# Strip runs of the value product that go on from one key group to the next

## The chip, the cores and the metric

The kernel runs on one core of a Trainium2 chip. The metric is the time of one execution in microseconds (us), measured on the device; of several runs the median is given. A profiled execution of the same program gives the trace: start and duration of every instruction on TensorE (PE, with its weight loads as PEld), VectorE (DVE), ScalarE (ACT), GpSimd (POOL) and the queues of the DMA issuers (SP above all).

## The reference, cut to what matters

Two sequences of 1024 positions with 1024 features pass a feed-forward layer with eight low-rank experts, a causal attention layer, and the same feed-forward layer again, each behind a layer norm and added to its input:

```python
x = x + 0.5 * ffn(layernorm(x))
x = x + attn(layernorm(x))
x = x + 0.5 * ffn(layernorm(x))

# attn: 32 query heads of 32 features, 8 key/value groups, 4 query heads to a group
att    = einsum('bhgqd,bhkd->bhgqk', q, k) / sqrt(32)     # rotary positions on q and k
att    = where(causal, att, -inf)
probs  = softmax(att)
ctx    = einsum('bhgqk,bhkd->bhgqd', probs, v)
out    = ctx @ Wo
```

The change lies in `ctx`, the product of the probabilities with the values, and in the row sums of the softmax.

## The kernel before

Positions are cut into 16 tiles of 128, numbered t = 0 to 15, eight to a sequence. A query tile t meets L = t % 8 + 1 key tiles of its own sequence. The 8 key/value groups are handled in four pairs, an even group and the odd one after it. Tile 8 (LATE, with L = 1) is worked on last.

For a query tile and a group, `unit_s1` (L650, with a mask in L655 for small L) computes scores with queries on the partitions, and DVE takes row maxima (L667). For a pair of groups the maxima are folded into the query operand: for L above 3 by writing them to columns of `qst` (L687, L688) and transposing on the DMA queue of SP (`qt_load`, L630); for L up to 3 by a small matmul (L697) and a DVE multiply (L699). `unit_s2` then computes the scores a second time with keys on the partitions, one matmul for a key tile and the four heads of the group (L809, result `s2`, 128x512). ACT takes the exponential into one of eight buffers `p32` (L815), and POOL clears the half above the diagonal for the last key tile (L817). These fp32 tiles feed the value product.

The value product (L745) uses strips of the PE array: for each head of the group a 128x32 weight (the values of the group, or a column block of ones) is loaded into its own 32 columns of the array, and the head's 128x128 block of `p32` streams against it. The four heads' matmuls work side by side in the four column strips. I call these four matmuls a step; the trace shows each step as eight records, since an fp32 matmul is recorded twice. There are two kinds of step: with the values (`va`), one for each key tile; and with `ones`, which gives the row sums. To save `ones` steps, DVE first adds two `p32` tiles of the same group into a `pair` tile (L723), so that there is one `ones` step for two key tiles, and one for a key tile left over.

Steps are grouped in batches. `av_add` (L772) appends every exponential tile to the newest batch in `pend`; a batch is closed when it has four tiles (BATCH) or when the group changes. A batch is issued by `av_batch` (L726) once at least two tiles (SKEW) came after it: all its `va` steps first, from the newest tile to the oldest, then its `ones` steps. All its matmuls but the first are chained with `issue_after` and a high priority, which keeps most of a batch together on PE. The sums of a pair of groups lie in one PSUM tile `av` with a single buffer; after the pair's last batch `normalize` (L753) copies it out on ACT (L757) and DVE (L758 to L765) and writes the context rows, `tt`, with ACT (L767) and POOL (L768).

The dense layers (L409 to L411: three fp16 matmuls for the high and low halves, 128x512; L592 to L594 and L616 to L618 in the first tiles; L492 to L494 for the experts) are written as generators that the loops around `unit_s2` advance a piece at a time, so that dense work lies between the attention work. Their weights stream from DRAM into three `ws` buffers (L421), and their inputs come by DMA transposes (`tt<-hl`, L338). The final order on each engine is set by the framework's own planner, which starts from the order of the program, priorities and `issue_after`. PE, DVE, ACT, POOL and SP each then run their list in order.

With four tiles to a batch, closed at the end of each group, a query tile has 8 batches for L up to 4 and 16 for L from 5 to 8: 192 in all.

Of the kernel before, what the change touches and what calls it, by code (L numbers as in the profile page):

```python
# [9 lines left out]
FP = mybir.dt.float32  # L10
# [3 lines left out]
ALU = mybir.AluOpType  # L14
# [3 lines left out]
NH, NKV, DH, GRP = 32, 8, 32, 4  # L18
E, R = 8, 16
P = 128  # L20
KB = D // P
NT = B * T // P
TPB = T // P
# [7 lines left out]
BATCH = 4  # L31
# [13 lines left out]
def kernel(  # L45
# [16 lines left out]
    nc = tc.nc  # L62
# [42 lines left out]
    ones = const.tile([P, DH], FP)  # L105
# [432 lines left out]
    KT, VA, QS, CTX, CT = {}, {}, {}, {}, {}  # L538
# [166 lines left out]
    pend = deque()  # L705
    ready = {}
    avt = [None]

    pairs = {}

    def add_pairs(batch):

        t, g, L, us = batch
        key = (t, g, us[0][0])
        if key in pairs:
            return
        pairs[key] = []
        for i in range(0, len(us), 2):
            if i + 1 == len(us):
                pairs[key].append(us[i][1])  # L720
                continue
            sums = pp.tile([P, GRP, P], FP, name="pair", bufs=3)
            nc.vector.tensor_tensor(sums, us[i][1], us[i + 1][1], ALU.add)  # L723
            pairs[key].append(sums)

    def av_batch():  # L726

        add_pairs(pend[0])
        t, g, L, us = pend.popleft()
        odd = g % 2  # L730
        if us[0][0] == 0 and not odd:
            avt[0] = p_av.tile([P, 2, 2, P], FP, name="av")
        av = avt[0][:, odd]
        last = us[-1][0] == L - 1
        runs = [(0, VA[t - t % TPB + j][:, g, :], p32) for j, p32 in reversed(us)]
        runs += [(1, ones, sums) for sums in reversed(pairs.pop((t, g, us[0][0])))]
        prev = None
        for n, (i, w, p32) in enumerate(runs):
            for h in range(GRP):
                rows = slice(h * DH, (h + 1) * DH)  # L740
                with ExitStack() as st:
                    if prev is not None:
                        st.enter_context(tc.high_priority())
                        st.enter_context(tc.issue_after(prev.ins))
                    prev = nc.tensor.matmul(  # L745
                        av[rows, i, :], lhsT=w, rhs=p32[:, h, :],
                        start=(us[0][0] == 0 and n == 0), stop=(last and n == len(runs) - 1),
                        skip_group_check=True, tile_position=(0, h * DH),
                    )
        if last and odd:  # L750
            normalize(t, g - 1, avt[0])

    def normalize(t, g, av):  # L753

        w = pp.tile([P, GRP, P], FP, name="pair", bufs=3)
        o, rc = w[:, 0:2, :], w[:, 2:4, :]
        nc.scalar.copy(o, av[:, :, 0, :])  # L757
        nc.vector.transpose(rc, av[:, :, 1, :])  # L758
        r = small.tile([P, 2 * P // DH], FP, name="rcol")
        nc.vector.reciprocal(r, rc.rearrange("p a (b q) -> p (a b) q", q=DH)[:, :, 0])  # L760
        nc.vector.transpose(rc, r.unsqueeze(2).to_broadcast([P, 2 * P // DH, DH]))
        if t not in CTX:
            CTX[t] = Halves()
        c = CTX[t]
        nc.vector.tensor_tensor(o, o, rc, ALU.mult)  # L765
        hi, lo = c.tt[:, g : g + 2, :], c.tt[:, KB + g : KB + g + 2, :]
        nc.scalar.copy(hi, o)  # L767
        nc.gpsimd.tensor_tensor(lo, o, hi, ALU.subtract)  # L768
        if g == NKV - 2:
            CT[t] = CTX.pop(t)  # L770

    def av_add(t, g, j, L, p32):  # L772

        if not pend or len(pend[-1][3]) == BATCH or pend[-1][0:2] != (t, g):
            pend.append((t, g, L, []))
        pend[-1][3].append((j, p32))
        after = 0
        while len(pend) > 1:
            after = sum(len(b[3]) for b in list(pend)[1:])
            add_pairs(pend[0])  # L780
            if after < SKEW:
                break
            av_batch()
# [15 lines left out]
    def unit_s2(t, g):  # L799
        b0 = t - t % TPB  # L800
        L = t - b0 + 1
        odd = g % 2
        while ("q2", t, g - odd) not in Ts:
            turn_maxima()
        q = (Ts.pop if odd else Ts.get)(("q2", t, g - odd))[:, odd * GRP : (odd + 1) * GRP, :]
        cs = S["cs", g // 4]
        for j in range(L):
            ps = p_s2.tile([P, GRP, P], FP, name="s2")
            ins = nc.tensor.matmul(  # L809
                ps.rearrange("p h k -> p (h k)"), lhsT=KT[b0 + j][:, g, :],  # L810
                rhs=q.rearrange("p h k -> p (h k)"), start=True, stop=True,
            )
            s2_ins.append(ins.ins)
            p32 = pp.tile([P, GRP, P], FP, name="p32", bufs=8)
            nc.scalar.activation(p32, ps, AF.Exp, scale=cs)  # L815
            if j == L - 1:
                nc.gpsimd.affine_select(  # L817
                    out=p32, in_=p32, compare_op=ALU.is_ge, fill=0.0, base=0,
                    pattern=[[0, GRP], [1, P]], channel_multiplier=-1,
                )  # L820
            av_add(t, g, j, L, p32)
            yield

    def stage_c1(t):
        while t not in CT:
            av_batch()
        tt = CT.pop(t)
        xt = xts[t]
        for n in range(2):
            ps = p_dense.tile([P, 512], FP, name="pd")  # L830
            yield from dense_streamed(ps, tt, 3 + n)
            c = bass.ts(n, 512)
            nc.vector.scalar_tensor_tensor(xt[:, c], ps, S["uo", n], xt[:, c], ALU.mult, ALU.add)
            if n == 0:
                yield True
        Ts["x3", t] = layernorm(xt, turn=t in TURN3)
        yield True
# [103 lines left out]
    def flush(_):  # L941
        while pend:
            av_batch()
        yield True
# [144 lines left out]
    pp = ctx.enter_context(tc.tile_pool(name="pp", bufs=2, reuse_waits="tile"))  # L1089
# [69 lines left out]
```

## Time and profile before

| | |
|---|---|
| median of 3 runs | 1469.46 us (1466.78 to 1469.99) |
| profiled execution | 1466.47 us |
| its span in the trace | 1464.6 us |
| mean granted TensorE clock | 0.989 |
| PE / DVE / ACT / POOL busy | 95% / 74% / 49% / 25% of the span |
| strip matmuls (L745), records | 4608 with `va`, 2048 with `ones` on a `pair`, 512 with `ones` on a single tile |
| the same in steps of eight records | 576, 256 and 64 |
| DVE pair sums (L723) | 256, mean 708 ns |
| exponentials (L815) | 576, mean 687 ns |

A PE matmul's record is longer than the time to the next one, since matmuls are pipelined; what a matmul costs is the distance from its start to the start of the next. In a list of groups a row has the line, engine, operation, output and inputs, shapes, count, busy time, mean duration, and the idle time before it with what ended it. In a timeline a row has the start, the time covered, and how many records in a row were merged.

### The profile page before, as it was taken

How to read it: one execution, taken by the hardware profiler on the slowest of the kernel's cores; microseconds unless marked ns; L12 is line 12 of the kernel's file. 1: busy time of each engine (PE TensorE's matmuls, PEld its weight loads, DVE VectorE, ACT ScalarE, POOL GpSimd, SP SyncE). 2: the span in 40 equal slices, each digit the busy share in tenths (PEclk: the TensorE clock that was granted, in tenths of full speed). 3: DMA queues.
4: the chain of work that ended last, by engine and by line, in shares of the span. 5: the costliest groups of instructions: out<-in, count | busy, mean ns of one | idle time of the engine just before them, and what ended most of it. 6: DMA issues, size and time to landing. Idle time of an engine off the chain costs nothing.

```text
span 1464.6 us, 35179 instructions
## 1 busy us (share of the span) xinstructions
PE 1392.4 (95%) x14636; PEld 786.9 (54%) x14636; DVE 1084.9 (74%) x2416; ACT 720.2 (49%) x1233; POOL 369.3 (25%) x578
## 2 busy tenths in 40 slices
PE   5897999999999999999999899999999999999998
PEld 3443445555556555556554455555555555556544
DVE  6878768968678687787754686868778688789743
ACT  7574434535456455464541343545545455555521
POOL 3352223323222131221211232322222122221220
PEclk9998999999999999999999999999999999999999
DMA  8958397585875837935649759697794855933552
GB/s 303 278 178 197 105 258 200 118 275 147 235 205 102 277 92 180 256 75 166 199 122 290 187 151 262 158 258 185 177 270 66 258 132 106 276 75 88 131 160 85
DMA packets 254863, 266.75 MB, mean 182 GB/s; under 512 B 217072, under 2 KB 220144, under 8 KB 234992
## 3 DMA queue, kind: packets, MB, share of 16 engines
q1 hardware_dynamic: 248624, 237.25, 58.0%
q0 software_dynamic: 4640, 16.78, 6.5%
q10 hardware_dynamic: 1440, 10.49, 2.0%
q8 instruction: 114, 1.87, 0.5%
q14 instruction: 45, 0.37, 0.1%
HBM read 191.60 MB, written 20.45 MB: 145 GB/s over the span
## 4 chain that ended last, share of the span: by engine, by line
PE 76%; DVE 11%; DMA 7%; issue 1%; ACT 1%; POOL 0%; SPq 0%; DVEq 0%; ACTq 0%; POOLq 0%
PE pd L409 15%; PE pd L410 15%; PE pd L411 14%; PE av L745 12%; PE s L809 7%; PE s L650 7%; DVE mx L667 4%; DMA qt<-qst 3%; DMA ws<-wstr 2%; DMA tt<-hl 2%; DVE pair L723 2%; DVE bst L379 1%; DVE xt L496 1%; PE pd L492 1%; PE pd L592 1%
## 5 line engine op out<-in xcount | busy, mean ns | idle before, releaser
L815 ACT ACTIVATE p<-s,cs 128x512 f32<-128x512 f32 x576 | 381.3, 687 | 299.7 <-PE s L809 297.1
L667 DVE TENSOR_REDUCE mx<-s 128x4 f32<-128x512 f32 x480 | 316.0, 677 | 43.2 <-PE s L650 39.1
L723 DVE TENSOR_TENSOR pair<-p,p 128x512 f32<-128x512 f32 x256 | 180.5, 708 | 69.1 <-ACT p L815 36.0
L650 PE MATMUL s<-kts,qt 96*128 96x128 f16 x2304 | 217.2, 221 | 6.1 <-DVE mx L667 3.1
L809 PE MATMUL s<-qt,kts 128*128 128x512 f16 x576 | 211.3, 384 | 10.5 <-DMA qt<-qst 7.0
L650 PEld LDWEIGHTS <-qt 96*128 96x128 f16 x2304 | 164.7, 98 | 97.4 <-issue 28.2
L409 PE MATMUL pd<-ws,tt 128*128 128x512 f16 x544 | 207.1, 381 | 9.2 <-DMA ws<-wstr 7.0
L410 PE MATMUL pd<-ws,tt 128*128 128x512 f16 x544 | 206.7, 380 | 0.0
L411 PE MATMUL pd<-ws,tt 128*128 128x512 f16 x544 | 206.6, 380 | 0.0
L409 PE MATMUL pd<-wb,tt 128*128 128x512 f16 x512 | 196.0, 383 | 2.4 <-DVE xt L496 1.5
L409 PEld LDWEIGHTS <-tt 128*128 128x128 f16 x1312 | 129.1, 98 | 127.3 <-DMA tt<-hl 12.6
L410 PE MATMUL pd<-wb,tt 128*128 128x512 f16 x512 | 195.6, 382 | 1.1 <-DVE wb L217 1.1
L411 PE MATMUL pd<-wb,tt 128*128 128x512 f16 x512 | 195.7, 382 | 0.0
L411 PEld LDWEIGHTS <-tt 128*128 128x128 f16 x1312 | 129.0, 98 | 121.8 <-issue 5.5
L410 PEld LDWEIGHTS <-tt 128*128 128x128 f16 x1312 | 129.2, 98 | 120.7 <-issue 15.2
L817 POOL TENSOR_SCALAR_AFFINE_SELECT p<-p 128x512 f32<-128x512 f32 x128 | 91.5, 717 | 347.2 <-ACT p L815 347.1
L745 PE MATMUL av<-p,va 128*32 128x128 f32 x4608 | 166.6, 278 | 1.4 <-POOL p L817 1.4
L745 PEld LDWEIGHTS av<-p,va 128*32 128x32 f32 x4608 | 115.7, 110 | 59.5 <-issue 42.4
L662 POOL TENSOR_SCALAR_AFFINE_SELECT sm<-sm 128x512 f32<-128x512 f32 x96 | 67.4, 702 | 159.6 <-ACT sm L661 154.0
L745 PE MATMUL av<-pair,ones 128*32 128x128 f32 x2048 | 86.8, 276 | 1.3 <-DVE pair L723 1.2
L661 ACT COPY sm<-s 128x512 f32<-128x512 f32 x96 | 56.0, 583 | 62.0 <-PE s L650 59.2
L527 POOL TENSOR_TENSOR t<-qs,sinT 128x256 f32<-128x256 f32 (+1 forms) x48 | 35.7, 745 | 185.9 <-ACT qs L518 184.8
(205 smaller groups left out, 1821.9 us busy)
## 6 DMA issues: line engine op xcount, KB each, us to landing
ws<-wstr SPq DMA_DIRECT2D x142, 1024.0 KB, 5.7
xt<-hb POOLq DMA_DIRECT2D x32, 512.0 KB, 6.3
wstr<-ws ACTq DMA_DIRECT2D x10, 1024.0 KB, 6.5
xt<-in_x_dram SPq DMA_DIRECT2D x16, 512.0 KB, 3.9
out_dram<-xt SPq DMA_DIRECT2D x15, 512.0 KB, 2.8
st<-in_wo_dram SPq DMA_DIRECT2D x3, 1024.0 KB, 10.9
ws<-in_wb_dram SPq DMA_DIRECT2D x2, 1024.0 KB, 8.3
qst<-in_wb_dram SPq DMA_DIRECT2D x2, 1024.0 KB, 12.6
```

Of the source, the lines that this page charges most:

```text
L409: nc.tensor.matmul(ps, lhsT=th, rhs=wh, start=(k == 0), stop=False)
L410: nc.tensor.matmul(ps, lhsT=th, rhs=wl, start=False, stop=False)
L411: nc.tensor.matmul(ps, lhsT=tl, rhs=wh, start=False, stop=(last and k == KB - 1))
L650: nc.tensor.matmul(ps[:, h, :], lhsT=q[0 : 3 * DH, h, :], rhs=KT[b0 + j][0 : 3 * DH, g, :], start=(not pem or h == 0), stop=not pem,)
L661: nc.scalar.copy(sm, ps)
L662: nc.gpsimd.affine_select(out=sm, in_=sm, compare_op=ALU.is_ge, fill=-3.0e38, base=0, pattern=[[0, GRP], [-1, P]], channel_multiplier=1,)
L667: nc.vector.tensor_reduce(mx[:, odd, j, :], ps, AX.X, ALU.max)
L723: nc.vector.tensor_tensor(sums, us[i][1], us[i + 1][1], ALU.add)
L745: prev = nc.tensor.matmul(av[rows, i, :], lhsT=w, rhs=p32[:, h, :], start=(us[0][0] == 0 and n == 0), stop=(last and n == len(runs) - 1), ...
L809: ins = nc.tensor.matmul(ps.rearrange("p h k -> p (h k)"), lhsT=KT[b0 + j][:, g, :], rhs=q.rearrange("p h k -> p (h k)"), start=True, stop ...
L815: nc.scalar.activation(p32, ps, AF.Exp, scale=cs)
L817: nc.gpsimd.affine_select(out=p32, in_=p32, compare_op=ALU.is_ge, fill=0.0, base=0, pattern=[[0, GRP], [1, P]], channel_multiplier=-1,)
```

## The change

A batch no longer ends with the group. It is keyed by the pair of groups, takes four tiles regardless of which group they belong to, and each tile carries its group with it. A pair sum is still made of two neighbouring tiles of one group only. Within a batch all `va` steps come first (newest tile first), then all `ones` steps, now of both groups. The start flag is set on the first matmul of the pair's first batch only, and `normalize` follows the batch that holds the odd group's last tile.

```diff
     def add_pairs(batch):
-        t, g, L, us = batch
-        key = (t, g, us[0][0])
+        t, _, _, us = batch
+        key = (t, *us[0][0:2])
         if key in pairs:
             return
         pairs[key] = []
-        for i in range(0, len(us), 2):
-            if i + 1 == len(us):
-                pairs[key].append(us[i][1])
-                continue
-            sums = pp.tile([P, GRP, P], FP, name="pair", bufs=3)
-            nc.vector.tensor_tensor(sums, us[i][1], us[i + 1][1], ALU.add)
-            pairs[key].append(sums)
+        i = 0
+        while i < len(us):
+            g, _, p32 = us[i]
+            i += 1
+            if i < len(us) and us[i][0] == g:
+                sums = pp.tile([P, GRP, P], FP, name="pair", bufs=3)
+                nc.vector.tensor_tensor(sums, p32, us[i][2], ALU.add)
+                p32 = sums
+                i += 1
+            pairs[key].append((g, p32))
 
     def av_batch():
         add_pairs(pend[0])
         t, g, L, us = pend.popleft()
-        odd = g % 2
-        if us[0][0] == 0 and not odd:
+        first, last = us[0][0:2] == (g, 0), us[-1][0:2] == (g + 1, L - 1)
+        if first:
             avt[0] = p_av.tile([P, 2, 2, P], FP, name="av")
-        av = avt[0][:, odd]
-        last = us[-1][0] == L - 1
-        runs = [(0, VA[t - t % TPB + j][:, g, :], p32) for j, p32 in reversed(us)]
-        runs += [(1, ones, sums) for sums in reversed(pairs.pop((t, g, us[0][0])))]
+        av = avt[0]
+        runs = [(u - g, 0, VA[t - t % TPB + j][:, u, :], p32) for u, j, p32 in reversed(us)]
+        runs += [(u - g, 1, ones, sums) for u, sums in reversed(pairs.pop((t, *us[0][0:2])))]
...
-                        av[rows, i, :], lhsT=w, rhs=p32[:, h, :],
-                        start=(us[0][0] == 0 and n == 0), stop=(last and n == len(runs) - 1),
+                        av[rows, a, i, :], lhsT=w, rhs=p32[:, h, :],
+                        start=(first and n == 0), stop=(last and n == len(runs) - 1),
...
-        if last and odd:
-            normalize(t, g - 1, avt[0])
+        if last:
+            normalize(t, g, av)
...
     def av_add(t, g, j, L, p32):
-        if not pend or len(pend[-1][3]) == BATCH or pend[-1][0:2] != (t, g):
-            pend.append((t, g, L, []))
-        pend[-1][3].append((j, p32))
+        pair = g - g % 2
+        if not pend or len(pend[-1][3]) == BATCH or pend[-1][0:2] != (t, pair):
+            pend.append((t, pair, L, []))
+        pend[-1][3].append((g, j, p32))
```

More of the change, by code (lines that the diff above doesn't have):

```diff
@@ L729, in av_batch @@
         t, g, L, us = pend.popleft()
-        odd = g % 2
-        if us[0][0] == 0 and not odd:
+        first, last = us[0][0:2] == (g, 0), us[-1][0:2] == (g + 1, L - 1)
+        if first:
             avt[0] = p_av.tile([P, 2, 2, P], FP, name="av")
-        av = avt[0][:, odd]
-        last = us[-1][0] == L - 1
-        runs = [(0, VA[t - t % TPB + j][:, g, :], p32) for j, p32 in reversed(us)]
-        runs += [(1, ones, sums) for sums in reversed(pairs.pop((t, g, us[0][0])))]
+        av = avt[0]
+        runs = [(u - g, 0, VA[t - t % TPB + j][:, u, :], p32) for u, j, p32 in reversed(us)]
+        runs += [(u - g, 1, ones, sums) for u, sums in reversed(pairs.pop((t, *us[0][0:2])))]
         prev = None
-        for n, (i, w, p32) in enumerate(runs):
+        for n, (a, i, w, p32) in enumerate(runs):
             for h in range(GRP):
```

## The prediction

> **What bounds the kernel now.** I read the engine shares and the clock first, then the waits of PE, then the groups of the value product, and last the timeline round a few strip runs.
>
> ```profile
> span 1464.6 us, 35179 instructions
> PE 1392.4 (95%) x14636; PEld 786.9 (54%) x14636; DVE 1084.9 (74%) x2416; ACT 720.2 (49%) x1233; POOL 369.3 (25%) x578
> PE   5897999999999999999999899999999999999998
> PEclk9998999999999999999999999999999999999999
> ```
>
> PE is busy in nine tenths or more of nearly every slice after the first four, at a granted clock of 0.9 or more but for one slice. What PE saves there shortens the execution; where it waits, a saving can go into the wait. How full it is by stage (busy time of each engine):
>
> ```profile
> 0.00:150.00 150.00, 119.69 (x715) 65.21 (x716) 113.86 (x286) 92.80 (x141) 56.06 (x107) 0.95 0.80 242
> 150.00:230.00 80.00, 75.91 (x618) 37.51 (x620) 57.01 (x121) 32.56 (x59) 25.12 (x38) 1.00 0.69 181
> 330.00:800.00 470.00, 463.54 (x5243) 266.81 (x5241) 345.84 (x758) 235.13 (x403) 103.37 (x158) 1.00 0.65 178
> 800.00:880.00 80.00, 72.81 (x570) 38.18 (x569) 59.16 (x136) 31.28 (x54) 20.77 (x33) 0.96 0.68 184
> ```
>
> The first column after the width is PE: 99% full from 330 to 800 us, 95% and 91% where tiles 1 and 9 (L = 2) are worked on. The waits of PE on attention work:
>
> ```profile
> PE s L809 <- DMA qt<-qst: 7.0, 8, 1.6
> PE s L809 <- ACT p L815: 3.3, 10, 0.7
> PE s L650 <- DVE mx L667: 3.1, 7, 1.3
> PE av L745 <- POOL p L817: 1.4, 3, 0.8
> PE av L745 <- DVE pair L723: 1.2, 3, 0.7
> ```
>
> The largest, 7.0 us in eight stops, is for the query operand that carries the maxima. Waits of the strip runs themselves are 2.6 us in all. Their work:
>
> ```profile
> L745 PE MATMUL av<-p,va 128*32 128x128 f32 x4608 | 166.6, 278 | 1.4 <-POOL p L817 1.4
> L745 PE MATMUL av<-pair,ones 128*32 128x128 f32 x2048 | 86.8, 276 | 1.3 <-DVE pair L723 1.2
> L745 PE MATMUL av<-p,ones 128*32 128x128 f32 x512 | 26.2, 277 | 0.0
> ```
>
> A single batch of two key tiles, in the timeline of PE:
>
> ```profile
> 186.15 0.38 PE L593 MATMUL pd<-ws,tt 128*128 128x512 f16 x1
> 186.36 0.38 PE L594 MATMUL pd<-ws,tt 128*128 128x512 f16 x1
> 186.67 0.65 PE L745 MATMUL av<-p,va 128*32 128x128 f32 x16
> 187.13 0.40 PE L745 MATMUL av<-pair,ones 128*32 128x128 f32 x8
> 187.47 0.39 PE L592 MATMUL pd<-ws,tt 128*128 128x512 f16 x1
> 187.69 0.38 PE L593 MATMUL pd<-ws,tt 128*128 128x512 f16 x1
> ```
>
> Dense matmuls start every 0.215 us (186.15, 186.36; 187.47, 187.69). A strip step inside a run takes 0.218 us (the usual distance between steps in the trace). From the last dense matmul before the run to the first one after it 1.11 us pass; 0.215 of it is that dense matmul and 3 x 0.218 = 0.654 the three steps. So 0.24 us is lost: some 0.09 going in (0.31 instead of 0.215) and some 0.15 coming out (0.34 for the last step instead of 0.218, and a little inside). Runs of one, two, four and six steps give the same 0.24. It is paid once for each stretch of strip matmuls, however long.
>
> **The change part by part.** *Work.* The number of matmuls is the same: 576 va steps, and still 256 + 64 ones steps. For odd L a pair of groups has two leftover tiles before and after (L = 3: three tiles and three become four and two; the pairs are again 0+1 of the first group and 1+2 of the second). DVE keeps its 256 sums of 0.708 us, ACT its 576 exponentials, SP and POOL their DMAs. Dropping the odd group's start flag changes no instruction. These cost nothing.
>
> *Stretches.* Batches go from 192 to 160: for L = 1 to 8 a tile now has 4, 4, 8, 8, 12, 12, 16, 16 of them instead of 8, 8, 8, 8, 16, 16, 16, 16. What is paid for is stretches on PE, and the built order has 225 of these before (some batches are split, with their ones steps set apart behind other matmuls; some follow each other directly) and 199 after. 26 fewer x 0.24 = 6.2 us. [...]
>
> *Where they fall.* By tile: 0 and 8: -2 and 0; 1 and 9: -5 and -4; 4 and 12: -1 and -1; 5 and 13: -8 and -7; 6: +4; 14: -3; 15: +1; the rest 0. So 11 of the 26 lie in stages with L up to 2, where PE is 91 to 95% full and meets fixed waits soon after. Lower bound of their worth 0, upper 11 x 0.24 = 2.6; I take half, 1.3, since these stages are still nearer to full than empty. The other 15 count in full: 3.6. Together -4.9 us.
>
> *Waits of the runs.* A run of four stands behind its newest tile, and all PE work behind the run stands with it. From the start of a tile's L809 to the tile's release I need some 0.45 + 0.69 (L815) + 0.70 (L817 with its handover, on the diagonal) = 1.9 us. Counting the distances along both orders with the trace's steps, before has shortfalls at tiles 1, 2, 9 and 14; after has them at tiles 1, 2, 9, 13 and 14. The worst new one is the first pair of tile 9: the run of four starts 0.3 us behind the L809 of its last tile, short by 1.6, and its sum by a little more; in the same place before there were two runs, which stopped PE 0.8 and 0.8 us (823 to 826 us). Shortfalls net: +0.5 (bounds -1, all in stages that wait anyway, and +3, each repeated by the sum behind it). [...]
>
> *Buffers.* Tiles wait longer in p32. Eight buffers are there; the shortest distance between the run that frees a buffer and the L809 whose exponential takes it was 0.3 us, and is -1.0 at one place of tile 14 (near 1285 us), where ACT will be up to 1 us late and the second L809 behind it too: +0.5 (0 to 1). The single av tile: the shortest gap from a pair's last step to the next pair's first is 1.9 us (1.8 before), against a copy of 0.37 (L757) and a transpose of 0.44 (L758): nothing.
>
> *Maxima.* All engines' lists shift. For each pair with L above 3, I take the PE time between the last L650 and the first L809, less the DVE work in the list from the last L667 to L688. PE stopped where this margin was 3.5 us or less: tile 3 first pair 3.5 (stop 1.3), 5 and 13 first 3.0 (0.4, 1.7), 6 first 3.3 (0.9), 7 first 1.0 (1.6), 14 first 3.5 (0.4), 14 last -0.4 (1.3), 15 second 2.7 (0.4): 8.0 with small change. In the new lists the same places have 4.7, 5.9, 5.9, 1.1, 2.7, 2.2, 1.9 and 3.2, and tile 3's second pair falls from 7.6 to 2.5. Priced by their neighbours: 0 + 0 + 0 + 1.6 + 0.9 + 1.2 + 1.2 + 0.4 + 1.2 = 6.5, so -1.5; bounds -4 and +4, since a moved DVE list is only roughly known. I take -0.5. Waits of L809 and L650 for a free PSUM tile have the same tightness in both lists: 0 (-2 to +2).
>
> Sum: -4.9 + 0.5 + 0.5 - 0.5 = -4.4 us. The profiled execution would go from 1466.47 (span 1464.6 and 1.9 around it) to about 1462. It lies 3.0 us under the median of the runs; from the median 1469.46 - 4.4 gives 1465.0.
>
> **The rivals.** *The saving is absorbed.* PE is rid of the entries and exits, but the next wait takes what is saved: DMA of weights (7.0 us in 4 stops) and of inputs, maxima, exponentials. For it: 11 of the 26 stretches lie where PE waits. Against it: from 330 to 800 us PE idles 6.5 us in 470. With only the 15 others, and the shortfalls and buffers at their upper ends (+4), -3.6 + 4 = about 0: 1469.5; more likely -1.5, 1468.
>
> *Late maxima, slower.* The place is the L809 behind qt<-qst at the first pairs of tiles with L from 4 to 7. If the moved sums and maxima make the DVE list late by about one sum (0.7 us) plus one L667 (0.68) at each of the nine tight places, and PE stops for it, this is 9 x 1.4 = 12 us more: 1465 + 12 = 1477. It decides from 7.3 us on (4.4 lost and 2.9 to be measurable), that is, when today's 7.0 us of such waits double. For it: DVE is 74% busy from 330 to 800 us (345.84 of 470) and the margins are a few us. Against it: six of the eight old tight places gain margin.
>
> *More than counted.* All 26 stretches pay in full (-6.2) and the maxima go to their better end (-3): 1460.
>
> *The change does not do what it says.* The planner could split the longer runs and leave 225 stretches; the built order shows 199, so this one is out, unless a stretch in it costs more than 0.24 because it now alternates between groups; the weights change with every step anyway, before as well.
>
> **How the numbers follow.** 0.2%, or 2.9 us, is about what a measurement tells from no change. Main case 0.50 (1465.0, its own range 1462 to 1467); more than counted 0.10 (1460); absorbed 0.25 (1468, some of it just past the bound of 1466.5); late maxima 0.15 (1473 to 1477, less when in part). Faster 0.60, same 0.25, slower 0.15. The range from 1459 to 1471 leaves out half of the late maxima and the far end of the better case.
>
> **What would show it.** In the profile after: the value product's records unchanged in number (4608, 2048, 512) and 256 sums; 199 stretches; the same 0.24 us for a stretch; PE busy lower by 5 to 6 us; waits of L809 on qt<-qst near 6.5 us; a stop of 1 to 2.5 us at the first run of tile 9. Wrong would be: the loss for a stretch growing with its length or with two groups in it; waits for qt<-qst of 12 us or more; waits of the strip runs well over 2.6 + 1 us; or a larger wait for weights (ws<-wstr) that no distance here shows.

## The result and the profile after

The changed kernel takes 1479.12 us (median of ten runs, 1469.45 to 1486.34). The kernel before, run beside it, takes 1467.26 (ten runs, 1463.96 to 1473.38). The ratio is 1.0081, 95% interval 1.0062 to 1.0101: slower by 0.8%, some 12 us. The prediction had 1465.0 with a range from 1459 to 1471, and gave "slower" a chance of 0.15: a change of -4.4 us was forecast, and the medians moved by +11.9.

The profiled execution after took 1480.88 us, with a span of 1479.1: 14.5 us more than the span before (1464.6). These are single executions: the one before lies 0.8 us under its median, the one after 1.8 us over it, so that 2.6 of the 14.5 us are spread. The page after, the lines that answer to those shown of before:

```profile
span 1479.1 us, 35179 instructions
PE 1391.8 (94%) x14636; PEld 792.0 (54%) x14636; DVE 1082.1 (73%) x2416; ACT 719.4 (49%) x1233; POOL 365.9 (25%) x578
PE   5897998899999999999999899999999999999997
PEclk9998999999999999999999999999999999999999
```

The number of instructions is the same, 35179, and so is that of matmuls, 14636. PE is as busy as before (1391.8 against 1392.4 us) in a span that is 14.5 us longer, so PE stands idle for longer. By stage, in the windows whose rows for before stand in the prediction (PE is the first column after the width):

```profile
0.00:150.00 150.00, 118.57 (x718) 64.86 (x719) 114.09 (x288) 92.84 (x141) 55.52 (x107) 0.94 0.77 242
150.00:230.00 80.00, 73.10 (x604) 37.88 (x606) 54.40 (x116) 30.87 (x57) 23.43 (x36) 1.00 0.71 183
330.00:800.00 470.00, 459.49 (x5253) 265.88 (x5251) 347.35 (x765) 235.29 (x404) 102.30 (x156) 0.99 0.65 172
800.00:880.00 80.00, 74.16 (x549) 39.27 (x548) 54.05 (x132) 26.60 (x47) 18.94 (x32) 0.96 0.74 203
```

From 330 to 800 us, the stretch that was 99% full, PE idles 10.5 us instead of 6.5. In tile 1's window (150 to 230 us) it idles 6.9 instead of 4.1. (The windows are the same times, not the same work: the changed kernel is 7 us behind near 330 us and 13 us near 811.) No single stage carries the loss.

The waits of PE after (total us, times, longest). The first row, `tt<-hl`, is the transposes that bring the dense layers' input; `ws<-wstr` is the streamed weights:

```profile
PE pd L409 <- DMA tt<-hl: 14.4, 9, 2.5
PE s L812 <- DMA qt<-qst: 13.1, 8, 2.4
PE pd L409 <- DMA ws<-wstr: 7.3, 7, 2.2
PE s L812 <- ACT p L818: 3.8, 12, 0.6
PE av L747 <- POOL p L820: 1.9, 2, 1.5
PE av L747 <- DVE pair L724: 0.7, 2, 0.5
PE s L650 <- DMA qt<-qst: 1.5, 2, 1.0
```

Before, the rows that the prediction did not show:

```profile
PE pd L409 <- DMA tt<-hl: 9.0, 6, 3.0
PE pd L409 <- DMA ws<-wstr: 7.0, 4, 3.3
PE s L650 <- DMA qt<-qst: 1.8, 3, 0.9
```

The strip runs' own waits are the two rows of L747: 2.6 us, exactly what they were before (1.4 + 1.2). What grew is the wait for two kinds of DMA transpose: `qt<-qst` from 8.8 to 14.6 us, with the rows of L650 counted in, and `tt<-hl` from 9.0 to 14.4.

The saving itself is there. A list of groups and, below it, the timeline of two runs:

```profile
L747 PE MATMUL av<-p,va 128*32 128x128 f32 x4608 | 161.0, 278 | 1.9 <-POOL p L820 1.9
L747 PE MATMUL av<-pair,ones 128*32 128x128 f32 x2048 | 86.4, 279 | 0.8 <-DVE pair L724 0.7
L747 PE MATMUL av<-p,ones 128*32 128x128 f32 x512 | 21.3, 273 | 0.0
```

```profile
181.69 0.38 PE L655 MATMUL s<-cmask,negid 128*128 128x512 f16 x1
182.00 1.08 PE L747 MATMUL av<-p,va 128*32 128x128 f32 x32
182.90 0.62 PE L747 MATMUL av<-pair,ones 128*32 128x128 f32 x16
183.45 0.39 PE L592 MATMUL pd<-ws,tt 128*128 128x512 f16 x1
...
351.89 0.38 PE L812 MATMUL s<-qt,kts 128*128 128x512 f16 x1
352.20 1.08 PE L747 MATMUL av<-p,va 128*32 128x128 f32 x32
353.10 0.62 PE L747 MATMUL av<-pair,ones 128*32 128x128 f32 x16
353.65 0.40 PE L650 MATMUL s<-kts,qt 96*128 96x128 f16 x4
```

The first run is one of tile 1 (L = 2), so its four `va` steps come from both groups; the second is in a stage with one group to a run. Both take 1.76 us from the start of the full-width matmul ahead to the start of the one behind: 0.215 + 6 x 0.218 = 1.52, and 0.24 for going in and out. A stretch with two groups in it costs no more than one with a single group. There are 199 stretches in the trace, as the order had it.

To part work from waiting I add up, along each kernel's PE order, the distances from start to start that the trace of before shows for each kind of matmul where nothing waits, with 0.24 us for a stretch. I call the sum "work" and the rest of the span "waits". Before, work is 1357.6 us and the rest 107.0; some 13.5 of these lie ahead of PE's first matmul and behind its last, and 93.5 are left as waits between. After, it is 1352.5 and 113.0. So work fell by 5.1 us and waits rose by 19.5. (26 stretches at 0.24 would be 6.2; the sums are good to one or two us.) Of these 19.5 the rows of the waits give 15.4: `qt<-qst` 5.8, `tt<-hl` 5.4, waits for DVE 2.6, for ACT 0.8, for POOL 0.5, for weights 0.3. Some 2 us more are dense matmuls that ran at half pace (0.43 us apart instead of 0.215) just after a stop: from 150 us on there are 27 of them instead of 12, some 3 us more (last section), and ahead of 150 us 11 instead of 17. The last 2 us are not assigned.

### The profile page after: what moved, and what is told of

Read it like the earlier page. It is cut to its first block, busy times and chain, and to the rows that moved or that the text cites. A ratio compares the mean times of both kernels' runs of the same rounds, so it can differ in the third digit from the quotient of the medians.

```text
span 1479.1 us, 35179 instructions
## 1 busy us (share of the span) xinstructions
PE 1391.8 (94%) x14636; PEld 792.0 (54%) x14636; DVE 1082.1 (73%) x2416; ACT 719.4 (49%) x1233; POOL 365.9 (25%) x578
## 4 chain that ended last, share of the span: by engine, by line
PE 69%; DVE 11%; DMA 10%; ACT 2%; issue 2%; SPq 1%; POOL 1%; ACTq 0%; DVEq 0%; POOLq 0%
PE pd L409 13%; PE pd L410 13%; PE pd L411 13%; PE av L747 11%; PE s L812 7%; PE s L650 7%; DMA qt<-qst 4%; DVE mx L667 4%; DMA ws<-wstr 3%; DMA tt<-hl 3%; DVE pair L724 1%; ACT p L818 1%; PE pd L492 1%; DVE xt L496 1%; PE pd L493 1%
## 5 line engine op out<-in xcount | busy, mean ns | idle before, releaser
L812 PE MATMUL s<-qt,kts 128*128 128x512 f16 x576 | 210.6, 384 | 17.0 <-DMA qt<-qst 13.1
L650 PE MATMUL s<-kts,qt 96*128 96x128 f16 x2304 | 218.9, 221 | 5.4 <-DVE mx L667 1.8
L650 PEld LDWEIGHTS <-qt 96*128 96x128 f16 x2304 | 167.1, 99 | 101.8 <-issue 30.2
L410 PEld LDWEIGHTS <-tt 128*128 128x128 f16 x1312 | 129.8, 99 | 119.2 <-issue 15.5
L747 PE MATMUL av<-p,va 128*32 128x128 f32 x4608 | 161.0, 278 | 1.9 <-POOL p L820 1.9
L747 PEld LDWEIGHTS av<-p,va 128*32 128x32 f32 x4608 | 117.1, 110 | 53.5 <-issue 38.9
L747 PE MATMUL av<-pair,ones 128*32 128x128 f32 x2048 | 86.4, 279 | 0.8 <-DVE pair L724 0.7
```

Of the source, the lines that this page charges most:

```text
L410: nc.tensor.matmul(ps, lhsT=th, rhs=wl, start=False, stop=False)
L650: nc.tensor.matmul(ps[:, h, :], lhsT=q[0 : 3 * DH, h, :], rhs=KT[b0 + j][0 : 3 * DH, g, :], start=(not pem or h == 0), stop=not pem,)
L747: prev = nc.tensor.matmul(av[rows, a, i, :], lhsT=w, rhs=p32[:, h, :], start=(first and n == 0), stop=(last and n == len(runs) - 1), skip_ ...
L812: ins = nc.tensor.matmul(ps.rearrange("p h k -> p (h k)"), lhsT=KT[b0 + j][:, g, :], rhs=q.rearrange("p h k -> p (h k)"), start=True, stop ...
```

## The experiments

The question is what raises the waits. Four explanations were tried: strip runs of four hold up PE behind their newest tile; the transposes land late because they meet another transfer; the new order of all the engines' lists costs, whether runs are joined or not; and a single kind of tile is to blame. "Saved" in the tables counts stretches against the 225 of before, "waits" is as above (93.5 before).

**One kind of tile at a time.** `av_add` keys the batch by the pair only for some L, and by the group for the rest; `e = g - g % 2` takes the place of `g` in `av_batch` where a pair is meant. The first three:

```diff
-        pair = g - g % 2
+        pair = g - g % 2 if L <= 2 else g        # or: L in (5, 6), L in (3, 7)
```

> Runs go on across groups only for tiles with L = 1 and 2. Its built order has 213 stretches of strip steps on PE (225 before, 199 in the changed kernel), so 12 fewer, worth -2.8 us at 0.235 us each. Theory A (late transposes: the saving is real, and the loss is made by the lists of all engines being planned anew, so that query and input transposes come late in tiles 1 to 6): the lists outside tiles 0, 1, 8 and 9 are nearly those of before, so the waits in tiles 3 to 6 stay as before, and the time is -4 to +2 us from before. Theory B (long mixed runs: a run that joins two groups stops PE behind its newest tile or keeps buffers too long, wherever it is used): waits grow by 3 to 5 us in tiles 1 and 9, and the time is 0 to +3 us from before.

> Runs go on across groups only for tiles with L = 5 and 6 (tiles 4, 5, 12, 13). 208 stretches, 17 fewer than before, worth -4.0 us. Theory A: the waits come where transposes are late, in any later tile and in tile 4's last pair (2 us each at tiles 4 and 12 in the changed kernel); time -4 to +8 us from before, and most of any loss is in PE's waits for qt<-qst and tt<-hl. Theory B: waits grow in tiles 4, 5, 12 and 13 alone, by 2 to 3 us each, time +4 to +8 us, and the waits name the strip runs or the exponentials.

> Runs go on across groups only for tiles with L = 3 and 7 (tiles 2, 6, 10, 14), where the number of batches does not fall: 231 stretches, 6 more than before, +1.4 us. Theory A: the sign is open, since lists are planned anew from tile 2 on: -3 to +10 us, with the difference from +1.4 in waits for transposes. Theory B: slower by 4 to 8 us, in tiles 2, 6, 10 and 14 alone.

**No joined run, but another order.** The kernel before with the `ones` steps of a batch taken oldest first. The steps of PE are the same in number and kind; only their order changes, and with it the planner's lists:

```diff
-        runs += [(1, ones, sums) for sums in reversed(pairs.pop((t, g, us[0][0])))]
+        runs += [(1, ones, sums) for sums in pairs.pop((t, g, us[0][0]))]
```

> The kernel before, with no run across groups; only the ones steps of a batch are issued oldest first instead of newest first. Same work; the built order has 218 stretches, 7 fewer than before (-1.6 us), and is planned anew from tile 3 on. Theory A: waits for transposes move by several us in either direction, so the time may be anywhere from -6 to +8 us from before, and a difference from -1.6 of over 3 us speaks for A. Theory B: no mixed runs, so no loss: -3 to 0 us.

Measured in one group (before there: 1468.53):

| joined for | median us | ratio (interval) | saved | waits |
|---|---|---|---|---|
| L = 1, 2 | 1469.56 | 1.0005 (0.9984 to 1.0026) | 12 | 93.7 |
| L = 5, 6 | 1476.54 | 1.0056 (1.0033 to 1.0080) | 17 | 103.6 |
| L = 3, 7 | 1470.98 | 1.0025 (1.0005 to 1.0045) | -6 | 102.2 |
| none, `ones` oldest first | 1473.62 | 1.0033 (1.0010 to 1.0056) | 7 | 101.1 |

A row's median stands for all its runs, but its waits are those of one execution, the profiled one. That lay 5.2 us under the median for L = 1, 2, 3.4 under it for L = 5, 6, 5.8 over it for L = 3, 7 and 0.5 under it in the last row; in the later tables it lies up to 7.5 us off. Differences of some 5 us between waits of different kernels therefore show little by themselves.

The 12 stretches saved at L = 1 and 2 bring nothing and cost nothing that can be measured. L = 5 and 6 carry the most, 8 us. And the fourth kernel, which joins nothing, loses 5 us: its PE work is 1.4 us less, its waits 7.6 us more. In its list of PE's waits:

```profile
PE pd L409 <- DMA tt<-hl: 11.5, 7, 3.2
PE pd L409 <- DMA ws<-wstr: 10.5, 7, 4.3
PE s L809 <- DMA qt<-qst: 8.4, 8, 1.8
```

Here `tt<-hl` (9.0 before) and the weights (7.0 before) rose most, and the maxima little (7.0 before). So a new order alone, with no joined run in it, makes PE wait longer for transfers. Joining is not needed for a loss of this size (5 us; its interval reaches from 1.5 to 8.2).

**Where the transposes land late.** Tile 4 of the kernel after (L = 5). Its timeline, with SP's queue (a duration there is how long the issue held the queue):

```profile
427.98 4.61 SPq L630 DMA_TRANSPOSE qt<-qst  x1
432.68 9.91 SPq L338 DMA_TRANSPOSE tt<-hl  x1
439.76 0.39 PE L650 MATMUL s<-kts,qt 96*128 96x128 f16 x4
442.01 0.38 PE L812 MATMUL s<-qt,kts 128*128 128x512 f16 x1 [1.86 <-DMA qt<-qst]
```

and how long the `qt` transposes took from issue to landing in the window from 410 to 435 us, after (the 3.0 is an earlier transpose, issued at 414.5 us):

```profile
DMA to landing us min/median/max: 3.0/15.0/15.3
```

and before:

```profile
DMA to landing us min/median/max: 6.5/8.1/9.6
```

POOL issues a DMA at 426.91 us that adds a bias of 1024 columns to `xt` (L447, `xt<-hb`, 512 KB). It and the two transposes landed at almost the same time, 442 to 443 us, and SP was held for 9.91 us by the transpose behind them. The order of these issues is the same before, but there the bias landed after 9 us and nothing waited. One difference stands in the traces: how soon the bias follows the first of the two transposes. After, 0.22 us:

```profile
426.69 5.90 SPq L630 DMA_TRANSPOSE qt<-qst  x2
426.91 0.95 POOL L447 DMA_DIRECT2D xt<-hb  x1 [0.71 <-ACT xn L400]
```

and before, 0.96 us:

```profile
420.34 5.18 SPq L630 DMA_TRANSPOSE qt<-qst  x2
421.30 0.95 POOL L447 DMA_DIRECT2D xt<-hb  x1 [1.59 <-ACT xn L400]
```

In the changed kernel tile 12, 670 us later, does the same (15.4 us, a stop of 2.35). If the bias transfer is what holds them, cutting it should undo it. In both kernels:

```diff
-        nc.gpsimd.dma_start(out=xt, in_=hb.partition_broadcast(P), accum_op=ALU.add)
+        nc.gpsimd.dma_start(out=xt[:, 0:8], in_=hb[0:8].partition_broadcast(P), accum_op=ALU.add)
```

> The changed kernel with the accumulating bias DMA of POOL (xt<-hb, 512 KB each, 32 times) cut to 8 of its 1024 columns; the bias is left out of the other columns. The lists of all engines are nearly those of the changed kernel. Theory C (contention: the late transposes share the DMA engines with the bias DMA, as at tile 4's last pair, where a transpose took 15 us beside it): the transposes at tiles 4 and 12 land within 9 us, PE's waits for qt<-qst fall from 13 to about 7 us and for tt<-hl from 14 to about 9 us, and the time falls by 8 us or more, to 1471 or less. Theory D (order alone: transposes are issued late because DVE and SP lists put them late): waits fall by 2 to 4 us, no more than in the kernel before.

> The kernel before with the same cut of the bias DMA, and nearly its own lists. Theory C: it gains little, 1 to 3 us, since its transposes are rarely beside a bias DMA, so that the changed kernel with the cut is as fast as this one or up to 4 us faster. Theory D: it gains the same 2 to 4 us as the changed kernel, and the changed kernel with the cut stays 8 to 12 us slower than this one.

Beside them the changed kernel once more, for a second trace, and joining at L = 1, 2, 5 and 6:

> The changed kernel once more, for a second trace. If the new waits belong to the lists, the same stops come back at tiles 3, 4, 12 and 14 within 0.7 us each, and the waits for qt<-qst and tt<-hl are again 5 us or more above those of before. If they were chance of one execution, they stand elsewhere.

> Runs go on only where that saves batches (L = 1, 2, 5, 6). 197 stretches, 28 fewer than before, worth -6.6 us. Theory A: -6.6 and the change in waits, which is that of a new plan: -6 to +8 us from before. Theory B: the sum of the runs with L up to 2 alone and with L = 5 and 6 alone.

| kernel (before here: 1467.99) | median us | ratio (interval) | saved | waits |
|---|---|---|---|---|
| after, bias cut | 1460.15 | 0.9948 (0.9929 to 0.9967) | 25 | 91.4 |
| before, bias cut | 1456.49 | 0.9916 (0.9895 to 0.9938) | 0 | 86.3 |
| after, again | 1478.62 | 1.0061 (1.0033 to 1.0089) | 26 | 110.8 |
| joined for L = 1, 2, 5, 6 | 1482.91 | 1.0108 (1.0072 to 1.0145) | 28 | 115.3 |

The waits of PE for transposes with the bias cut, after:

```profile
PE s L812 <- DMA qt<-qst: 8.2, 6, 2.1
PE pd L409 <- DMA tt<-hl: 7.2, 5, 2.2
```

and before:

```profile
PE s L809 <- DMA qt<-qst: 8.0, 8, 2.1
PE pd L409 <- DMA tt<-hl: 4.2, 3, 1.7
```

The bias transfer costs both kernels: the one before 11.5 us, where 1 to 3 had been expected, and the one after 18.5. Without it the transposes at tile 4 land after 7.6 us (median) in the changed kernel too, and its waits fall by 21.6 (7.2 before). The distance between the two falls from 10.6 us to 3.7. That is what a collision would do, though the two distances are not firmly apart: each is known to some 4 us. And 3.7 us are left, where a gain of 5 was due. Joining at L = 1, 2, 5 and 6 loses 14.9 us, more than either theory allowed (at most 8, or the 1.0 and 8.0 of the two parts added).

The second trace of the kernel after shows the same places: `qt<-qst` 12.6 us, `tt<-hl` 13.2, stops of 2.04 us at tile 4 and 2.89 at tile 12. They are a property of the kernel, not of one execution. Two tries to lessen the collision followed. One issues the bias in two halves of 512 columns, each written ahead of its half of the next dense layer. They were meant to come some 5 us apart, but the planner put them together: in both traces the second follows the first by 0.5 to 1.1 us. So the bytes go in two transfers, but hardly spread over time. The other leaves the bias whole and loads 64 columns of each weight block only:

```diff
-        nc.gpsimd.dma_start(out=xt, in_=hb.partition_broadcast(P), accum_op=ALU.add)
...
+            hc = bass.ts(n, 512)
+            nc.gpsimd.dma_start(out=xt[:, hc], in_=hb[hc].partition_broadcast(P), accum_op=ALU.add)
```

```diff
-            nc.sync.dma_start(out=w, in_=wstr[ci, h])
+            nc.sync.dma_start(out=w[:, :, :, 0:64], in_=wstr[ci, h][:, :, :, 0:64])
```

> The changed kernel with each bias DMA split into two of 512 columns, the second issued some 5 us later, beside the second half of the dense layer. Same bytes. 197 stretches. Contention: a burst of the bias DMA is halved, so a transpose beside it lands within 10 us and the time falls by 4 to 10 us, to 1468 to 1475; if it is only the total of bytes that counts, the time stays within 3 us of 1478. All lists are planned anew, which may add or take some 5 us.

> The kernel before with the same split. 220 stretches. Its transposes took at most 12 us beside a bias DMA, so it gains less than the changed kernel: -3 to +6 us from 1468, with a new plan of all lists in it.

> The changed kernel with the repeated loads of the streamed weights cut to 64 of 512 columns, so that most weights are stale; the bias DMA is whole. 201 stretches. If all contention of DMAs made the loss, the time falls by 10 us or more, to 1468 or less. If the loss is the bias DMA's alone, transposes beside it still take over 12 us at tiles 4 and 12, and the time falls by no more than the kernel before with the same cut does, some 5 to 7 us (its waits for ws<-wstr).

> The kernel before with the same cut of the weight loads. 224 stretches. It loses its 7 us of waits for weights and some of its 18 us for transposes: 1456 to 1463. The distance of the changed kernel with the cut from this one is +10 us if weights have no part in the loss, and -4 to 0 if they have the main part.

| kernel (before here: 1468.53) | median us | ratio (interval) | waits |
|---|---|---|---|
| after, bias in halves | 1478.79 | 1.0069 (1.0045 to 1.0093) | 115.6 |
| before, bias in halves | 1476.80 | 1.0058 (1.0034 to 1.0081) | 101.7 |
| after, short weights | 1464.62 | 0.9973 (0.9950 to 0.9995) | 101.1 |
| before, short weights | 1459.18 | 0.9935 (0.9912 to 0.9958) | 90.4 |

The halves mended the place and not the time. The transposes at tiles 4 and 12 still take 12.0 to 13.5 us, but PE no longer stops for them there; PE now waits 15.9 us for `tt<-hl` instead of 14.4, and the median is where it was. On the kernel before, the halves alone cost 8 us, again with no joined run, though here a DMA more for each bias is part of the change. The short weights, which leave most weight columns unloaded, make both kernels faster, by 14.5 and 9.3 us, and yet the transposes at tile 4 take 15.1 us in the changed one (5.9 at tile 12): the bulk of the weights is not needed for the late landing.

Set side by side, joining costs 10.6 to 11.9 us as the kernel stands, 3.7 with the bias cut, 2.0 with the bias in halves and 5.4 with short weights. The last three are single differences of two medians, each known to 4 to 5 us. All four have the same sign, and none shows the gain of 4.4 us that was forecast.

**L = 5 or L = 6.** Last, the costliest pair taken apart, and everything joined but L = 3, 5 and 7:

```diff
-        pair = g - g % 2
+        pair = g - g % 2 if L == 6 else g        # or: L == 5, L in (1, 2, 6)
```

> Runs go on across groups only for L = 6 (tiles 5 and 13). 212 stretches, 13 fewer than before, worth -3.1 us; the lists are those of before up to tile 5. If the loss at L = 5 (the collision of two query transposes, an input transpose and a bias DMA in tiles 4 and 12) is the main part of that of the L = 5 and 6 kernel (+8 us), this one is -3 to +2 us from before, with no transpose over 13 us at tiles 4 and 12. If any new plan costs as much, +3 to +8 us.

> Runs go on only for L = 5 (tiles 4 and 12). 217 stretches, 8 fewer, worth -1.9 us. If the collision comes with the runs at L = 5, transposes of 14 to 16 us stand at tiles 4 and 12 again, PE stops 2 us at each, and the time is +2 to +7 us from before. If it comes from the combination with other tiles, no transpose is over 13 us there and the time is -2 to +5 us.

> Runs go on for L = 1, 2 and 6. 201 stretches, 24 fewer, worth -5.6 us. If leaving out L = 5 is enough, -5 to 0 us from before and this is the version to keep; if any new plan costs waits for transposes, 0 to +8 us.

| joined for (before here: 1468.34) | median us | ratio (interval) | saved | waits | `qt` landing at tile 4 / 12, median us |
|---|---|---|---|---|---|
| L = 6 | 1471.13 | 1.0018 (0.9996 to 1.0040) | 13 | 100.7 | 8.0 / 8.0 |
| L = 5 | 1473.41 | 1.0028 (1.0004 to 1.0052) | 8 | 94.6 | 14.4 / 15.5 |
| L = 1, 2, 6 | 1477.09 | 1.0057 (1.0037 to 1.0078) | 24 | 109.4 | 6.4 / 6.8 |

The profiled execution for L = 5 took 1465.94 us, the quickest of its twelve runs, so its waits of 94.6 stand for less than the median.

The late landing belongs to joining at L = 5. It is there in each kernel that joins these runs with the bias and the weights whole: after and its second trace, L = 5 and 6 (14.9 / 15.8), L = 1, 2, 5, 6 (15.1 / 14.1), L = 5 alone. In the kernels that don't, the same transposes take 11.5 us at most, mostly 6 to 9. PE then stops 1.2 to 2.9 us at each of the two places: 3.0 us together with L = 5 alone, 4.2 after. But joining at L = 1, 2 and 6 loses 8.7 us with no late landing at all. By the stops that name it the collision is one part of the loss, and not the larger one.

The distance of the bias goes with this without exception. In all ten places at tiles 4 and 12 of the five traces that join L = 5, with bias and weights whole, the bias is issued 0.23 us behind the first transpose, and the two transposes take 14.1 to 16.3 us. In all twelve places of the six traces that don't, it is issued 0.96 us behind, and they take 6.0 to 11.5. Two places speak against the distance as the whole cause: in the changed kernel with short weights, at 0.03 us, tile 4 has 15.1 us and tile 12 has 5.9; and with the `ones` oldest first, where nothing is joined, a transpose near 1003 us takes 16.0 us beside a bias that came 1.1 us behind the transpose ahead. No run moves the bias alone, so the distance is a sign of the late landing and not shown to be its cause.

**Where the rest is.** The remaining waits are many small ones. The sums of the waits by tile, one trace to a kernel, show that they sit in part at the joined tiles themselves and come back in different kernels:

| tile (L) | waits where its runs are joined, us | where not, us |
|---|---|---|
| 1 (2) | 7.3 to 8.5 | 3.2 to 5.1 |
| 9 (2) | 7.4 to 9.0 | about 6.4 in four traces, 9 to 11 in two (L = 5; L = 3, 7) |
| 5 (6) | 3.3 to 5.2 | 2.0 to 3.0 |
| 13 (6) | 3.0 to 5.4 | 1.5 to 3.1 |
| 4 (5) | 2.3 to 4.3 | 0.8 to 1.0 |

With L = 5 and 6 joined, tiles 4, 5, 12 and 13 alone add 10.9 us of waits, and all tiles together 10.1. With L = 3 and 7 joined it is the reverse, and joining there saves no stretch: the joined tiles wait 5.2 us less, and tiles 8 and 9, which are not joined, 9 more.

What is settled: the stretches are saved; the strip runs themselves don't wait more; the time goes into more and longer stops for transposes, maxima and inputs, spread over the tiles, and the late landing at L = 5 gives 4 to 5 of the 19.5 us. What stays open are two things. The issues at tile 4 come in the same sequence before and after, 6 us later in the changed kernel, and no run shows why the landing takes 15 us instead of 9; the bias's distance is the difference to try first. And the part of the loss that belongs to joining as such can't be told from the part that any new order costs: two kernels without a joined run lose 5 and 8 us. No version that does all the work beats the kernel before; joining at L = 1 and 2 alone is level with it.

## Why the prediction was wrong

- **Stretches: right.** 199 were predicted and found, at 0.24 us each with one group or two. Work along the order fell by 5.1 us; the prediction counted 6.2 and took 4.9. PE's busy time was to fall by 5 to 6 us. It fell by 0.6 in the first trace (1391.8) and by 5.3 in the second (1387.1): busy time also holds the half-paced matmuls, of which the second trace has fewer (15 against 27 from 150 us on).
- **Waits of the strip runs: near.** +0.5 was taken, and it came out as 0 (2.6 us both times). The worst place was named rightly: the first run of tile 9 was to be short by 1.6 us, and it stops for 1.48 us where there were stops of 0.75 and 0.65.
- **Buffers: fits.** +0.5 was taken; waits of L812 behind ACT went from 3.3 to 3.8 us. No run tells whether the place near 1285 us is the cause.
- **Maxima: the step that failed.** -0.5 was taken, with bounds of -4 and +4; the waits for `qt<-qst` rose by 5.8 us. The step compared margins in the lists and left the transpose's own time as it was. Where the margins decide it was of use: the stops at the first pairs of tiles 3, 5 and 13 are gone as foreseen, and tile 3's second pair, where a new stop of 1.2 was foreseen, stops for 1.84. The places that were priced at 6.5 in all came to 8.9; tile 14's last pair is the worst, 2.43 us where 1.2 was taken. The other 4.2 us are two new stops, 1.86 and 2.35, at the last pairs of tiles 4 and 12, which had 14 us of margin by the same count and so no price. There the transposes took 15 us to land instead of 8.
- **The inputs of the dense layers: a missing term.** The sum had no step for `tt<-hl`, though it was PE's largest wait for a transfer (9.0 us) before. It went through the same queue of SP, beside the same bias transfer, and rose by 5.4 us. The other waits for DVE rose by 2.6 us, and the half pace after stops added 2 in this trace; neither had a term. Half pace does not make the loss: the second trace, with 15 such matmuls from 150 us on against the 12 of before, still spans 12.2 us more than before.
- **The absorbed saving, and late maxima.** The prediction gave half of 11 stretches for absorption; the runs with L = 1 and 2 alone, which save 12 stretches (2.9 us), came out at a ratio of 1.0005, and their interval reaches down to a gain of 2.4 us: the gain is likely absorbed whole. The rival "late maxima" named the right wait and the right sign ("waits for qt<-qst of 12 us or more" would be the mark of error, and 13.1 were measured). Its price of 1.4 us at each of nine places rested on a late DVE list, and that is not what happened: a late landing at two places gives 4.2 us of the growth. By itself the rival would have given 1473 to 1477; the time is higher since inputs, DVE and the clock came on top, so that it came as near as it did in part by luck.

The sum by what was measured: -5.1 for the work, +5.8 `qt<-qst`, +5.4 `tt<-hl`, +4.2 for other rows of the waits, +2 at half pace and +2 not assigned: +14.3 in the traces, against the 14.5 between the two spans.

## What to carry to other kernels

On this engine, 95% full, a saving spread in pieces of 0.24 us was worth less than the order that it was bought with. Where all lists move, put the term "transfers land at other times" in the sum, bound it by a kernel that only reorders (here 5 us, as much as the saving), and let the range reach that far. Give every transfer that PE already waits for its own term, and don't hold its landing time fixed when the issues beside it move. To judge such a change, run an order-only variant beside it, better several, since otherwise the price of a new order is taken for the price of the idea.

## What the runs showed of the hardware

**Two transposes took 15 us instead of 8 in the same company.** The `qt` transposes took 3.0 us at best, at tile 4 6.5 to 9.6 us beside the bias transfer before, and 15 us beside it after, with the same issues in the same order. After, they and the bias land within 1.1 us of each other, and the queue that issues them is held for 9.91 us by the transpose behind. Removing 1016 of the bias's 1024 columns took 11.5 us from the kernel before, though no row of PE's waits names it: part of what it cost stood in the waits for `tt<-hl`, which fell from 9.0 to 4.2 us.

**PE ran at half pace for 3 us after one stop, and at full pace after a longer one at the same place.** In the timeline of the kernel after:

```profile
887.04 0.61 PE L650 MATMUL s<-kts,qt 96*128 96x128 f16 x8
889.88 0.61 PE L409 MATMUL pd<-ws,tt 128*128 128x512 f16 x1 [2.23 <-DMA tt<-hl]
890.28 0.63 PE L410 MATMUL pd<-ws,tt 128*128 128x512 f16 x1
...
892.84 0.51 PE L410 MATMUL pd<-ws,tt 128*128 128x512 f16 x1
893.19 0.38 PE L411 MATMUL pd<-ws,tt 128*128 128x512 f16 x1
893.41 0.38 PE L409 MATMUL pd<-ws,tt 128*128 128x512 f16 x1
```

After a stop of 2.23 us the dense matmuls start 0.43 us apart for 3 us, and 0.215 apart from then on. The granted clock is 0.50 from 889.7 to 893.1 us, and 1.00 ahead of it and behind it. In the second trace of the same kernel a stop of 2.44 us at the same place has no such tail, and the dense matmuls behind it start 0.22 us apart from the first on:

```profile
887.83 0.39 PE L409 MATMUL pd<-ws,tt 128*128 128x512 f16 x1 [2.44 <-DMA tt<-hl]
888.05 0.38 PE L410 MATMUL pd<-ws,tt 128*128 128x512 f16 x1
888.27 0.38 PE L411 MATMUL pd<-ws,tt 128*128 128x512 f16 x1
```

From 150 us on the first trace after holds 27 such half-paced matmuls, the second 15, before 12; the mean granted clock of the three is 0.984, 0.988 and 0.989. What decides whether a stop has such a tail is not shown: the stop that had it, 2.23 us, was the shorter of the two, and in the 3.7 us ahead of the tail PE was busy for 1.66.

**The spread was wider after.** The ten runs of the kernel after lie between 1469 and 1486 us, and seven later ones between 1470 and 1487. The ten of before lie between 1464 and 1473, and larger groups of it, 28 to 35 runs, between 1462 and 1477.
